# Two graph layers in float32: attention with the sources on the partitions, layer 0 as (attn @ h) @ W, one batch per group

## The chip, the cores and the metric

The kernel runs on one core of a Trainium2 chip. The time is that of the device, in microseconds, from launch to end. All data are float32. A core has TensorE (PE, matmuls; PEld is its weight load), VectorE (DVE), ScalarE (ACT), GpSimd (POOL) and SyncE (SP, here only the issue of DMAs). Each engine works through its own queue in order and waits at semaphores.

## The reference

x is 64 batches of 256 nodes with 512 features; adj (256 x 256) is shared by all batches. Both layers are pre-norm with a residual.

```python
# layer 0
h = relu(layernorm(x))
Wh = h @ W                                              # 512 x 512
logits = (Wh @ a_src)[:, :, None] + (Wh @ a_dst)[:, None, :]
logits = where(logits >= 0, logits, 0.2 * logits)
attn = softmax(where(adj == 0, -inf, logits))           # over the sources
x = x + attn @ Wh
# layer 1, 8 heads of 64
h = relu(layernorm(x))
q, k, v = h @ Wq.T + bq, h @ Wk.T + bk, h @ Wv.T + bv
attn = softmax(where(adj == 0, -inf, q @ k.T / 8))      # per head
x = x + (attn @ v) @ Wo.T + bo
```

## The kernel before

A group is two batches, i.e. four tiles of 128 tokens (`GB = 2`, L53). Everything stays on chip between load and store.

`norm_relu_T` (L121) takes mean and variance on VectorE, raises to the power -0.5 on GpSimd (L132), normalises on VectorE (xn, L137), transposes on TensorE (pt, L142) and applies relu on ScalarE (hT, L143). `project_rows` (L150) and `project_T` (L157) are the dense products: four accumulating matmuls, each with 512 moving columns.

`layer0` makes Wh (pw, copied to wh), its two row products with a_src and a_dst on VectorE (junk, L174), the logits with the targets on the partitions (z, L190 to L193), the row maximum, exp with the row sum (L200), transposes the probabilities (pp, L214) and multiplies them with wh (po, L223).

`layer1` makes qT and kT with the features on the partitions and v with the tokens on them. Then, for each tile of 128 targets and each four heads, `scores` multiplies qT by kT (psc, L281; a head has 64 features, so even and odd heads lie on the two halves of the rows), adds the mask and takes the row maximum on VectorE (s, L292), and takes exp with the row sum on ScalarE (pr, L308). `values` transposes the four probabilities (pp, L322), copies them back (pT, L327 and L329) and multiplies each with 64 columns of v (pav, L333). `finish` divides by the row sum (rc, L344; av, L346), transposes again (pa, L354, aT, L356), multiplies with Wo and stores.

Order: the generators of `layer1(g)` and `layer0(g + 1)` are interleaved step by step (L391 to L394), and a scheduler at build time orders the instructions of each engine, TensorE's too, by priority and its own estimate of when they are ready. SP issues first the load of x for group 0 and then those of the weights. PSUM's eight banks are split 2 (dense products), 3 (transposes) and 3 (scores).

Of the kernel before, what the change touches and what calls it, by code (L numbers as in the profile page):

```python
# [1 line left out]

# [13 lines left out]
P = 128  # L16
# [4 lines left out]
FLOOR = -1.0e30  # L21


@with_exitstack
def kernel(
# [17 lines left out]
    """Two pre-norm residual layers over batches of N nodes, kept on chip between them:  # L43
    graph attention with additive logits, then masked multi-head attention.

    A group is two batches, i.e. NT = 4 tiles of 128 tokens; its first layer is issued
    among the second layer of the group before it.
    """
# [4 lines left out]
    GB = 2  # L53
# [8 lines left out]
    big = ctx.enter_context(tc.tile_pool(name="big", bufs=2))  # L62
    work = ctx.enter_context(tc.tile_pool(name="work", bufs=3))
    small = ctx.enter_context(tc.tile_pool(name="small", bufs=4))
    ps_mm = ctx.enter_context(tc.tile_pool(name="ps_mm", bufs=2, space=PSUM))
    ps_tr = ctx.enter_context(tc.tile_pool(name="ps_tr", bufs=3, space=PSUM))
    ps_sc = ctx.enter_context(tc.tile_pool(name="ps_sc", bufs=3, space=PSUM))
# [3 lines left out]

    def load_group(g):
        xt = big.tile([P, NT, D], F32, tag="x", name=f"x_{g}", bufs=3)
        src = x_rows[g * TOK : (g + 1) * TOK, :].rearrange("(t p) d -> p t d", p=P)
        for t in range(0, NT, 2):
            nc.sync.dma_start(xt[:, t : t + 2, :], src[:, t : t + 2, :])
        return xt

    groups = {0: load_group(0)}
# [17 lines left out]
    make_identity(nc, ident)  # L97
    minus_half = const.tile([P, NT], F32, tag="minus_half", name="minus_half")
# [3 lines left out]
    a_src_b = load_row(a_src, "a_src_b")  # L102
    a_dst_b = load_row(a_dst, "a_dst_b")
# [8 lines left out]
    bv_b = load_row(bv, "bv_b")  # L112
    bo_b = load_row(bo, "bo_b")

    # 0 where there is an edge, MASKED where there is none
    mbias = const.tile([P, NC, N], F32, tag="mbias", name="mbias")
    nc.vector.tensor_scalar(mbias, adj_sb, 0.0, MASKED, op0=ALU.is_equal, op1=ALU.mult)
# [3 lines left out]
    def norm_relu_T(xt, g, layer):  # L121
        """relu(layernorm(x)) with the features on the partitions: [P, DC, TOK]."""
        nm = f"{layer}_{g}"
        mv = small.tile([P, NT, 2], F32, tag="mv", name=f"mv{nm}")
        for t in range(NT):
            st = small.tile([P, 6], F32, tag="st", name=f"st{nm}_{t}")
            nc.vector.bn_stats(st, xt[:, t, :])
            nc.vector.bn_aggr(mv[:, t, :], st)
        ve = small.tile([P, NT], F32, tag="ve", name=f"ve{nm}")
        nc.vector.tensor_scalar_add(ve, mv[:, :, 1], EPS)  # L130
        rstd = small.tile([P, NT], F32, tag="rstd", name=f"rstd{nm}")
        nc.gpsimd.tensor_tensor(rstd, ve, minus_half, op=ALU.pow)  # L132
        yield
        hT = big.tile([P, DC, TOK], F32, tag="hT", name=f"hT{nm}")
        for t in range(NT):
            xn = work.tile([P, D], F32, tag="xn", name=f"xn{nm}_{t}")
            nc.vector.tensor_scalar(  # L137
                xn, xt[:, t, :], mv[:, t, 0:1], rstd[:, t : t + 1], op0=ALU.subtract, op1=ALU.mult
            )
            pt = ps_tr.tile([P, DC, P], F32, tag="tr", name=f"pt{nm}_{t}")  # L140
            for c in range(DC):
                nc.tensor.transpose(pt[:, c, :], xn[:, c * P : (c + 1) * P], ident)  # L142
            nc.scalar.activation(hT[:, :, t * P : (t + 1) * P], pt, AF.Relu)  # L143
            yield
        return hT

    def project_rows(dst, hT, w_t, t):
        """dst[tokens of tile t, all columns] = h @ w_t"""
# [5 lines left out]
    def project_T(dst, hT, w_t, e):  # L154
        """dst[columns of chunk e, all tokens] = (h @ w_t).T"""
# [5 lines left out]
    def layer0(g):  # L161
        xt = groups[g]
        hT = yield from norm_relu_T(xt, g, 0)

        wh = big.tile([P, NT, D], F32, tag="wh", name=f"wh_{g}")
        es = small.tile([P, NT], F32, tag="es", name=f"es_{g}")
        ed = small.tile([P, NT], F32, tag="ed", name=f"ed_{g}")
        for t in range(NT):
            pw = ps_mm.tile([P, D], F32, tag="mm", name=f"pw_{g}_{t}")
            project_rows(pw, hT, w_sb, t)  # L170
            nc.scalar.copy(wh[:, t, :], pw)  # L171
            for dst, a in ((ed, a_dst_b), (es, a_src_b)):
                junk = work.tile([P, D], F32, tag="junk", name=f"junk_{g}_{t}", bufs=2)
                nc.vector.scalar_tensor_tensor(  # L174
                    junk, wh[:, t, :], 1.0, a, op0=ALU.mult, op1=ALU.mult, accum_out=dst[:, t : t + 1]
                )
            yield

        prob, rec = {}, {}
        for b in range(GB):  # L180
            per = ps_tr.tile([P, N], F32, tag="tr", name=f"per_{g}_{b}")
            for c in range(NC):
                t = b * NC + c
                nc.tensor.transpose(
                    per[:, c * P : (c + 1) * P], ed[:, t : t + 1].to_broadcast([P, P]), ident
                )
            z = work.tile([P, NC, N], F32, tag="z", name=f"z_{g}_{b}", bufs=2)
            for c in range(NC):
                t = b * NC + c
                nc.vector.scalar_tensor_tensor(  # L190
                    z[:, c, :], per, es[:, t : t + 1], mbias[:, c, :], op0=ALU.add, op1=ALU.add
                )
            nc.vector.scalar_tensor_tensor(z, z, NEG_SLOPE, z, op0=ALU.mult, op1=ALU.max)  # L193
            nmx = small.tile([P, NC], F32, tag="nmx0", name=f"nmx0_{g}_{b}")
            nc.vector.tensor_reduce(nmx, z, AX.X, ALU.max)
            nc.vector.tensor_scalar(nmx, nmx, FLOOR, -1.0, op0=ALU.max, op1=ALU.mult)
            pr = work.tile([P, NC, N], F32, tag="pr0", name=f"pr0_{g}_{b}", bufs=2)
            sm = small.tile([P, NC], F32, tag="sm0", name=f"sm0_{g}_{b}")
            for c in range(NC):
                nc.scalar.activation(  # L200
                    pr[:, c, :], z[:, c, :], AF.Exp, bias=nmx[:, c : c + 1], accum_out=sm[:, c : c + 1]
                )
            # a row without an edge gives 0
            nc.vector.tensor_scalar_max(sm, sm, 1e-30)
            rc = small.tile([P, NC], F32, tag="rc0", name=f"rc0_{g}_{b}")
            nc.vector.reciprocal(rc, sm)
            prob[b], rec[b] = pr, rc
            yield

        for b in range(GB):  # L210
            pp = ps_tr.tile([P, NC, N], F32, tag="tr", name=f"pp0_{g}_{b}")
            for mc in range(NC):
                for c in range(NC):
                    nc.tensor.transpose(  # L214
                        pp[:, mc, c * P : (c + 1) * P], prob[b][:, c, mc * P : (mc + 1) * P], ident
                    )
            pT = work.tile([P, NC, N], F32, tag="pT0", name=f"pT0_{g}_{b}", bufs=2)
            nc.vector.tensor_copy(pT, pp)
            for c in range(NC):
                t = b * NC + c  # L220
                po = ps_mm.tile([P, D], F32, tag="mm", name=f"po0_{g}_{t}")
                for mc in range(NC):
                    nc.tensor.matmul(  # L223
                        po,
                        pT[:, mc, c * P : (c + 1) * P],
                        wh[:, b * NC + mc, :],
                        start=(mc == 0),
                        stop=(mc == NC - 1),
                    )
                nc.vector.scalar_tensor_tensor(  # L230
                    xt[:, t, :], po, rec[b][:, c : c + 1], xt[:, t, :], op0=ALU.mult, op1=ALU.add
                )
            yield

    def layer1(g):
        xt = groups.pop(g)
        hT = yield from norm_relu_T(xt, g, 1)
        for t in range(NT):
            nc.gpsimd.tensor_tensor(xt[:, t, :], xt[:, t, :], bo_b, op=ALU.add)

        qT = big.tile([P, DC, TOK], F32, tag="qT", name=f"qT_{g}", bufs=1)
        kT = big.tile([P, DC, TOK], F32, tag="kT", name=f"kT_{g}", bufs=1)
        v = big.tile([P, NT, D], F32, tag="v", name=f"v_{g}")
        for e in range(DC):
            pq = ps_mm.tile([P, TOK], F32, tag="mm", name=f"pq_{g}_{e}")
            project_T(pq, hT, wq_sb, e)
            nc.scalar.activation(
                qT[:, e, :], pq, AF.Identity, bias=bqs_c[:, e : e + 1], scale=SCALE
            )
            pk = ps_mm.tile([P, TOK], F32, tag="mm", name=f"pk_{g}_{e}")  # L250
# [174 lines left out]
```

## Time and profile before

| | |
|---|---|
| median of 3 runs | 3981.32 us (3980.46 to 3982.46) |
| span of the profiled execution | 3978.6 us |
| TensorE busy | 3853.1 us, 97% |
| VectorE busy | 1732.9 us, 44% |
| ScalarE busy | 1109.1 us, 28% |
| GpSimd busy | 247.8 us, 6% |
| mean granted TensorE clock | 0.998 |
| HBM | 40.11 MB read, 33.55 MB written, 19 GB/s over the span |

The profile is of one execution; its span runs from the first to the last instruction and is 2.7 us shorter than the median. Matmuls are pipelined, so the duration of one (592 ns for 512 columns) is longer than the distance between the starts of two; a price is read from starts, not from durations. A float32 matmul leaves two records, a transpose one.

### The profile page before, as it was taken

How to read it: one execution, taken by the hardware profiler on the slowest of the kernel's cores; microseconds unless marked ns; L12 is line 12 of the kernel's file. 1: busy time of each engine (PE TensorE's matmuls, PEld its weight loads, DVE VectorE, ACT ScalarE, POOL GpSimd, SP SyncE). 2: the span in 40 equal slices, each digit the busy share in tenths (PEclk: the TensorE clock that was granted, in tenths of full speed). 3: DMA queues.
4: the chain of work that ended last, by engine and by line, in shares of the span. 5: the costliest groups of instructions: out<-in, count | busy, mean ns of one | idle time of the engine just before them, and what ended most of it. 6: DMA issues, size and time to landing. Idle time of an engine off the chain costs nothing.

```text
span 3978.6 us, 41676 instructions
## 1 busy us (share of the span) xinstructions
PE 3853.1 (97%) x15744; PEld 2182.8 (55%) x15744; DVE 1732.9 (44%) x5186; ACT 1109.1 (28%) x3201; POOL 247.8 (6%) x206
## 2 busy tenths in 40 slices
PE   7999999999999999999999999999999999999999
PEld 3555555555555555555555555555555555555555
DVE  3444344443345433454334543344443444433442
ACT  1322223222233222332223322233222232222332
POOL 1000000000000000000000000000000000000000
PEclk9999999999999999999999999999999999999999
DMA  2000000000000000000000000000000000000000
GB/s 98 22 9 16 19 22 22 9 16 19 22 22 14 13 17 22 22 22 6 19 19 22 22 6 19 19 22 22 9 16 19 22 22 9 16 19 22 11 11 11
DMA packets 39144, 76.33 MB, mean 19 GB/s; under 512 B 3297, under 2 KB 3297, under 8 KB 38945
## 3 DMA queue, kind: packets, MB, share of 16 engines
q1 hardware_dynamic: 38480, 72.36, 5.0%
q8 instruction: 124, 2.03, 0.2%
q0 software_dynamic: 464, 1.32, 0.1%
q14 instruction: 76, 0.61, 0.1%
HBM read 40.11 MB, written 33.55 MB: 19 GB/s over the span
## 4 chain that ended last, share of the span: by engine, by line
PE 87%; DVE 9%; ACT 3%; issue 1%; DMA 0%; POOL 0%; POOLq 0%; DVEq 0%; ACTq 0%
PE pav L333 12%; PE po L150 12%; PE pq L157 11%; PE pw L150 11%; PE pv L150 11%; PE pk L157 11%; PE psc L281 5%; PE pp L322 5%; PE po L223 4%; ACT hT L143 2%; PE pa L354 2%; DVE s L292 2%; PE pt L142 2%; DVE av L346 2%; DVE x L230 1%; DVE junk L174 1%
## 5 line engine op out<-in xcount | busy, mean ns | idle before, releaser
L333 PEld LDWEIGHTS pav<-v,pT 128*128 128x128 f32 x4096 | 498.8, 191 | 136.5 <-issue 45.9
L308 ACT ACTIVATE pr<-s,nmx 128x256 f32<-128x256 f32 x1024 | 507.0, 497 | 180.1 <-DVE nmx L304 157.9
L333 PE MATMUL pav<-v,pT 128*128 128x64 f32 x4096 | 525.0, 276 | 6.9 <-DVE pT L329 4.8
L150 PE MATMUL po<-wo_sb,aT 128*128 128x512 f32 x1024 | 474.2, 606 | 3.2 <-ACT aT L356 0.7
L157 PE MATMUL pq<-hT,wq_sb 128*128 128x512 f32 x1024 | 463.6, 595 | 7.9 <-ACT hT L143 7.9
L157 PE MATMUL pk<-hT,wk_sb 128*128 128x512 f32 x1024 | 460.3, 592 | 0.0
L150 PE MATMUL pw<-w_sb,hT 128*128 128x512 f32 x1024 | 460.1, 592 | 0.0
L150 PE MATMUL pv<-wv_sb,hT 128*128 128x512 f32 x1024 | 444.7, 592 | 0.0
L252 DVE TENSOR_SCALAR kT<-pk,bk_c 128x512 f32<-128x512 f32 x128 | 96.1, 751 | 776.0 <-PE pk L157 776.0
L281 PE MATMUL psc<-kT,qT 64*128 64x256 f32 x2048 | 399.0, 413 | 8.4 <-DVE mx L292 6.4
L292 DVE CUSTOM_DVE_ANT_0 s<-psc,mbias 128x256 f32<-128x256 f32 x1024 | 384.3, 417 | 11.1 <-PE psc L281 6.8
L171 ACT COPY wh<-pw 128x512 f32<-128x512 f32 x128 | 74.9, 585 | 1100.2 <-PE pw L150 1100.2
L157 PEld LDWEIGHTS pk<-hT,wk_sb 128*128 128x128 f32 x1024 | 194.6, 190 | 244.9 <-issue 244.9
L150 PEld LDWEIGHTS pv<-wv_sb,hT 128*128 128x128 f32 x1024 | 194.6, 190 | 244.9 <-issue 244.9
L150 PEld LDWEIGHTS pw<-w_sb,hT 128*128 128x128 f32 x1024 | 194.7, 190 | 244.5 <-issue 244.5
L157 PEld LDWEIGHTS pq<-hT,wq_sb 128*128 128x128 f32 x1024 | 191.9, 190 | 245.2 <-issue 229.6
L322 PE MATMUL pp<-ident,pr 128*128 128x128 f32 x2048 | 311.6, 277 | 5.0
L327 ACT COPY pT<-pp 128x512 f32<-128x512 f32 x256 | 149.1, 582 | 581.1 <-PE pp L322 578.2
L150 PEld LDWEIGHTS po<-wo_sb,aT 128*128 128x128 f32 x1024 | 184.4, 190 | 217.3 <-issue 184.1
L322 PEld LDWEIGHTS pp<-ident,pr 128*128 128x128 f32 x2048 | 234.3, 145 | 83.6 <-issue 44.1
L281 PEld LDWEIGHTS psc<-kT,qT 64*128 64x128 f32 x2048 | 220.9, 185 | 100.1 <-issue 56.8
L174 DVE SCALAR_TENSOR_TENSOR junk<-wh,a_dst_b 128x512 f32<-128x512 f32 x128 | 88.5, 691 | 421.4 <-ACT wh L171 421.4
(57 smaller groups left out, 3103.3 us busy)
## 6 DMA issues: line engine op xcount, KB each, us to landing
x<-in_x_dram SPq DMA_DIRECT2D x64, 512.0 KB, 4.4
out_dram<-x SPq DMA_DIRECT2D x128, 256.0 KB, 2.0
w_sb<-in_L_gnn_W_dram SPq DMA_DIRECT2D x1, 1024.0 KB, 13.3
wq_sb<-in_L_gnn_Wq_dram SPq DMA_DIRECT2D x1, 1024.0 KB, 15.9
wk_sb<-in_L_gnn_Wk_dram SPq DMA_DIRECT2D x1, 1024.0 KB, 18.1
wv_sb<-in_L_gnn_Wv_dram SPq DMA_DIRECT2D x1, 1024.0 KB, 20.1
wo_sb<-in_L_gnn_Wo_dram SPq DMA_DIRECT2D x1, 1024.0 KB, 16.1
a_src_b<-in_L_gnn_a_src_dram POOLq DMA_DIRECT2D x1, 256.0 KB, 6.8
```

The costliest lines, as they stand in the source:

```text
L142: nc.tensor.transpose(pt[:, c, :], xn[:, c * P : (c + 1) * P], ident)
L150: nc.tensor.matmul(dst, hT[:, c, t * P : (t + 1) * P], w_t[:, c, :], start=(c == 0), stop=(c == DC - 1))
L157: nc.tensor.matmul(dst, w_t[:, c, e * P : (e + 1) * P], hT[:, c, :], start=(c == 0), stop=(c == DC - 1))
L174: nc.vector.scalar_tensor_tensor(junk, wh[:, t, :], 1.0, a, op0=ALU.mult, op1=ALU.mult, accum_out=dst[:, t : t + 1])
L223: nc.tensor.matmul(po, pT[:, mc, c * P : (c + 1) * P], wh[:, b * NC + mc, :], start=(mc == 0), stop=(mc == NC - 1),)
L252: nc.vector.tensor_scalar_add(kT[:, e, :], pk, bk_c[:, e : e + 1])
L281: nc.tensor.matmul(psc[r][:, i, :], qT[rows, e, t * P : (t + 1) * P], kT[rows, e, b * N : (b + 1) * N], start=True, stop=True,)
L292: nc.vector.tensor_tensor_reduce(out=s[:, j, :], in0=psc[r][:, i, :], in1=mbias[:, c, :], scale=1.0, scalar=FLOOR, op0=ALU.add, op1=ALU.ma ...
L308: nc.scalar.activation(pr[:, j, :], s[:, j, :], AF.Exp, bias=nmx[:, j : j + 1], accum_out=sm[:, h : h + 1])
L322: nc.tensor.transpose(pp[:, r, kc, :], pr[:, 2 * i + r, kc * P : (kc + 1) * P], ident)
L327: nc.scalar.copy(pT, pp)
L333: nc.tensor.matmul(pav[:, h * DH : (h + 1) * DH], pT[:, r, kc, :], v[:, b * NC + kc, h * DH : (h + 1) * DH], start=(kc == 0), stop=(kc == ...
```

## The change

- A group is one batch (`GB = 1`, 64 groups); the dense products with features on the partitions have 256 moving columns, those with tokens on them 512 as before.
- Layer 0: h keeps its tokens on the partitions. Its row products are taken with W @ a_src and W @ a_dst, which are made once. exp(leaky_relu(s + d)) is the larger of exp(s)exp(d) and exp(0.2 s)exp(0.2 d), so only vectors go through exp (xs, xd) and VectorE builds the matrix (e1, eb), sources on the partitions. GpSimd multiplies by the transposed mask (em) and adds the two halves (esum); a product with ones sums over the sources. uT = (attn @ h) transposed is the product of h and em, scaled by the reciprocal of the sums, and W comes last.
- Layer 1: scores are made with the sources on the partitions. No maximum is subtracted: exp on ScalarE straight from PSUM, times the mask on VectorE (pm), the two halves added on GpSimd (sm). `values` has v as the stationary operand and pm as the moving one, 256 columns; even heads go to rows 0 to 63 of the output and odd heads to 64 to 127, and the sums over the sources come from a product with ones into the same rows of another bank (psm). VectorE takes the reciprocal of 512 sums and multiplies. The result is already transposed for Wo. The bias bv is folded into bo once.
- A bound is computed from the weights (`constants`): powers of the heads' Gram matrices of Wq and Wk, the sizes of biases and of W @ a. It gives a flag, which goes through DRAM into a register; where it says that the bound doesn't hold, `general` computes everything again with row maxima, batch by batch.
- TensorE's instructions keep the order in which the program writes them (`manual_schedule`); the other engines are still ordered by the scheduler. The order is that of a planner over three generators: at each step it takes the stage with the smallest key, group + done/cost + offset. A yield carries the cost of its TensorE work.
- x of group 0 is loaded after the weights in SP's order. PSUM: four banks for dense products and transposes, two for scores, one each for pav and psm.

The core of the diff; new functions that the prediction doesn't need in full are cut.

```diff
+GB = 1
...
-    GB = 2
...
+        ps_mm = ctx_b.enter_context(tc.tile_pool(name="ps_mm", bufs=4, space=PSUM))
+        ps_sc = ctx_b.enter_context(tc.tile_pool(name="ps_sc", bufs=2, space=PSUM))
+        ps_av = ctx_b.enter_context(tc.tile_pool(name="ps_av", bufs=1, space=PSUM))
...
+        def layer0(g):
...
+            pe = bank([P, TOK], f"pe_{g}")
+            for t in range(NT):
...
+                    pe[:, t * P : (t + 1) * P], es[:, t : t + 1].to_broadcast([P, P]), ident
+                )
+            xs = work.tile([P, 2, TOK], F32, tag="xs", name=f"xs_{g}")
+            xd = small.tile([P, 2, NT], F32, tag="xd", name=f"xd_{g}")
+            for j, slope in enumerate((1.0, NEG_SLOPE)):
+                nc.scalar.activation(xd[:, j, :], ed, AF.Exp, scale=slope)
+                nc.scalar.activation(xs[:, j, :], pe, AF.Exp, scale=slope)
+            yield 0.25
...
+                    nc.vector.tensor_scalar_mul(e1, xs[:, 0, cols], xd[:, 0, t : t + 1])
+                    nc.vector.scalar_tensor_tensor(
+                        eb[:, m, :], xs[:, 1, cols], xd[:, 1, t : t + 1], e1, op0=ALU.mult, op1=ALU.max
+                    )
+                em[b] = work.tile([P, NC, N], F32, tag="em", name=f"em_{g}_{b}")
+                nc.gpsimd.tensor_tensor(em[b], eb, maskT, op=ALU.mult)
+                esum[b] = work.tile([P, N], F32, tag="esum", name=f"esum_{g}_{b}")
+                nc.gpsimd.tensor_tensor(esum[b], em[b][:, 0, :], em[b][:, 1, :], op=ALU.add)
+                yield 0.0
...
+            ps = bank([P, TOK], f"ps_{g}")
+            for b in range(GB):
+                nc.tensor.matmul(
+                    ps[:, b * N : (b + 1) * N], ones, esum[b], start=True, stop=True
+                )
+            nc.vector.tensor_scalar_max(rs, ps, 1e-38)
+            nc.vector.reciprocal(rs, rs)
+            yield 0.45
...
+                    yield 1.7
+            for t in range(NT):
+                po = bank([P, D], f"po0_{g}_{t}")
+                project_rows(po, uT, w_sb, t)
+                nc.vector.tensor_add(xt[:, t, :], po, xt[:, t, :])
+                yield 3.43
...
+        def attention(g):
...
+            def scores(b, e):
...
+                for m in range(NC):
+                    for r in range(2):
+                        rows = slice(r * DH, (r + 1) * DH)
+                        nc.tensor.matmul(
+                            psc[r][:, m, :],
+                            kT[rows, e, b * N + m * P : b * N + (m + 1) * P],
+                            qT[rows, e, b * N : (b + 1) * N],
...
+                for r in range(2):
+                    nc.scalar.activation(ex[:, r, :, :], psc[r], AF.Exp)
+                pm = work.tile([P, 2, NC, N], F32, tag="pm", name=f"pm_{g}_{b}_{e}")
+                for r in range(2):
+                    nc.vector.tensor_mul(pm[:, r, :, :], ex[:, r, :, :], maskT)
+                sm = work.tile([P, 2, N], F32, tag="sm", name=f"sm_{g}_{b}_{e}")
+                nc.gpsimd.tensor_tensor(sm, pm[:, :, 0, :], pm[:, :, 1, :], op=ALU.add)
...
+            def values(b, e):
+                pm, sm = probs.pop((b, e))
+                i = e % 2
...
+                for m in range(NC):
+                    for r in range(2):
+                        h = 2 * e + r
+                        nc.tensor.matmul(
+                            pav[r * DH : (r + 1) * DH, i, :],
+                            v[:, b * NC + m, h * DH : (h + 1) * DH],
+                            pm[:, r, m, :],
...
+                for r in range(2):
+                    nc.tensor.matmul(
+                        psm[r * DH : (r + 1) * DH, i, :],
+                        ones[:, 0:DH],
+                        sm[:, r, :],
...
+                if i == 0:
+                    return
...
+                rc = work.tile([P, 2, N], F32, tag="rc", name=f"rc_{g}_{b}_{e}")
+                nc.vector.reciprocal(rc, psm)
+                nc.vector.tensor_mul(aTs[b][:, e - 1 : e + 1, :], pav, rc)
...
+            for n, unit in enumerate(units):
+                scores(*unit)
+                yield 0.9
+                if late:
+                    late.pop(0)()
+                    yield 1.3 if n == 0 else 3.43
+                if n:
+                    values(*units[n - 1])
+                    yield 1.3
+            late.append(partial(values, *units[-1]))
+            late.extend(partial(finish, t) for t in range(NT))
...
+        stages = [
+            [layer0, 11.5, 0.0],
+            [projections, 21.5, 1.1],
+            [attention, 15.7, 2.2],
+        ]
+        state = [dict(g=0, gen=None, done=0.0) for _ in stages]
+        side = constants()
+        while any(s["g"] < G for s in state):
+            keys = []
+            for k, s in enumerate(state):
+                if s["g"] < G and (k == 0 or state[k - 1]["g"] > s["g"]):
+                    keys.append((s["g"] + s["done"] / stages[k][1] + stages[k][2], k))
+            _, k = min(keys)
+            s = state[k]
+            if s["gen"] is None:
+                s["gen"], s["done"] = stages[k][0](s["g"]), 0.0
+            cost = next(s["gen"], None)
+            if cost is None:
+                s["g"], s["gen"], s["done"] = s["g"] + 1, None, 0.0
+            else:
+                s["done"] += cost
...
+    with ExitStack() as ctx_b:
+        with tc.manual_schedule(engines={mybir.EngineType.PE}):
+            bounded()
+    flag_dram = dram.tile([1, 1], I32, tag="flag_dram", name="flag_dram")
+    nc.sync.dma_start(flag_dram, flag)
+    unproven = nc.values_load(flag_dram[0:1, 0:1], min_val=0, max_val=1)
+    with tc.If(unproven > 0):
+        with ExitStack() as ctx_g:
+            general()
```

`projections` runs the norm, the transposes pt, then q and k by turns in steps of 1.72 and v in steps of 3.43; its last pt and its first q follow one another.

## The prediction

> **What bounds the kernel now.** I read the page's busy line and chain first, then TensorE's timeline in one steady group, then single tiles.
>
> ```profile
> PE 3853.1 (97%) x15744; PEld 2182.8 (55%) x15744; DVE 1732.9 (44%) x5186; ACT 1109.1 (28%) x3201; POOL 247.8 (6%) x206
> PE 87%; DVE 9%; ACT 3%; issue 1%; DMA 0%; POOL 0%; POOLq 0%; DVEq 0%; ACTq 0%
> ```
>
> TensorE is busy 97% of 3978.6 us and is 87% of the chain. VectorE at 44% is far from being a bound, so the price list of TensorE counts. Its timeline (start, us, operation, count; two records per float32 matmul, one per transpose):
>
> ```profile
> 2006.99 1.09 PE L322 MATMUL pp<-ident,pr 128*128 128x128 f32 x8
> 2008.02 0.70 PE L281 MATMUL psc<-kT,qT 64*128 64x256 f32 x4
> 2008.65 2.00 PE L333 MATMUL pav<-v,pT 128*128 128x64 f32 x16
> 2010.58 0.70 PE L281 MATMUL psc<-kT,qT 64*128 64x256 f32 x4
> ...
> 2035.24 3.60 PE L157 MATMUL pk<-hT,wk_sb 128*128 128x512 f32 x8
> 2038.67 3.60 PE L157 MATMUL pq<-hT,wq_sb 128*128 128x512 f32 x8
> ```
> ```profile
> 59.97 3.70 PE L157 MATMUL pq<-hT,wq_sb 128*128 128x512 f32 x8 [0.23 <-ACT hT L143]
> ...
> 115.10 1.13 PE L281 MATMUL psc<-kT,qT 64*128 64x256 f32 x8
> 116.16 0.43 PE L184 MATMUL per<-ident,ed 128*128 128x128 f32 x2
> ```
> ```profile
> 3878.51 3.70 PE L157 MATMUL pq<-hT,wq_sb 128*128 128x512 f32 x8 [0.79 <-ACT hT L143]
> ```
>
> From start to start: 8 records of 512 columns take 3.43 us, **0.429 us** a record; so a 256-column record is 0.215 (half, an estimate). Transposes cost 1.03/8 = 0.13, elsewhere 0.11. A 64-column record costs 1.93/16 = **0.12**, not 0.054: moving only 64 columns wastes half. Scores on half the rows: four matmuls (8 records) take 116.16 - 115.10 = **1.06 us**, five units of 0.213 where one after another would be eight; two halves run beside each other, except that the first and the last record stand alone. The group period is (3878.51 - 59.97)/31 = 123.2 us, **61.6 us per batch**.
>
> **What the skill says.** "VectorE: DVE Perf Modes", First, the fixed hardware budget: reciprocal is an iterative divide with a repeat count of 8. The trace agrees: two elements take 156 ns and eight 202, so (202 - 156)/6 = 7.7 ns each, where other operations of 2 or 4 elements (L196, L304) differ by under 10.
>
> ```profile
> L344 DVE RECIPROCAL rc<-sm x128: 189/202/204, 128.7 to 3963.1; 128x8 f32<-128x8 f32 x128
> L206 DVE RECIPROCAL rc<-sm x64: 152/156/166, 36.8 to 3827.0; 128x2 f32<-128x2 f32 x64
> ```
>
> "TensorE: Matmul & The Clock Gate", What's actually happening: an idle window of about 3.4 us halves TensorE's clock, and a busy one restores it. The trace agrees (columns: window, length, TensorE busy, granted clock, DMA): idle from 32.1 to 36.12 but for one short transpose before, the clock falls at 33.9 and is back only at 40.7, 4.5 us after work resumed.
>
> ```profile
> 33.00:34.00 1.00, 0.00 (x0) 0.92 0.00 0
> ...
> 36.00:37.00 1.00, 0.86 (x3) 0.50 0.03 8
> ...
> 39.00:40.00 1.00, 1.00 (x2) 0.50 0.00 0
> 40.00:41.00 1.00, 1.00 (x3) 0.67 0.00 0
> ```
>
> The same page, Part 3, says that matmuls on separate column groups also run concurrently. No column group occurs in this trace; rows agree.
>
> **The change on TensorE, per batch.** Removed: the transposes of the probabilities (pp, pp0) and of av (pa), and 64-column matmuls.
> - Layer 0: 2 transposes 0.25; row sums 0.43; attn@h, 8 matmuls of 256 columns, 16 x 0.215 = 3.44; times W, 16 x 0.429 = 6.86. Sum 11.0.
> - Projections: 8 transposes 1.0; q and k, 64 records x 0.215 = 13.8; v 6.86. Sum 21.7.
> - Attention, four units. Scores: the shape measured above, 1.06. Values: six matmuls alternating between two column halves. Not shown before: if they pair as the row halves do, seven units of 0.213 = 1.49; perfect pairing gives 1.28, none 2.56. I take 1.49. Output 6.86. Sum 4 x 2.55 + 6.86 = 17.1.
> - Switching between shapes: entering a dense stream costs about 0.1 (2031.70 to 2035.24 is 3.54 for the first block, 3.43 for the next). Some ten entries: 1.0 (0 to 2).
>
> Together **50.8 us** against 61.6. If TensorE never waited, 64 batches would take 64 x 50.8 = 3251.
>
> **The waits it adds.** TensorE's order is now written by the planner, and TensorE is served in order. I followed its rule (smallest progress key) by hand through a period. It repeats: values of unit 1 (VA1), then at once the two transposes `pe` of a later batch, at once the row sum `ps`, then scores of unit 3, pu, pt, values of unit 2, pt, q. The zero-cost yields change no key, so nothing goes between `pe` and `ps`. But `ps` needs pe -> exp (ScalarE) -> e1, eb (VectorE) -> em, esum (GpSimd). Behind it are queued all matmuls of other stages, ready as they are.
>
> And VA1 ends with a reciprocal of 512 elements, which is written earlier and ready earlier than e1, so it stands first in VectorE's queue: 0.16 + 510 x 7.7 ns = 4.1 us. From VA1's end: pipeline and semaphore 0.25; reciprocal to 4.35; product with pav, 0.65 (row of av, L346, less its overlap with the next), to 5.0; two e1 and two eb of 256 elements, 1.5 together (between half of xn, L137, 0.54, and z, L190, 0.476), to 6.5; em on GpSimd at the row of L239, 1.39, to 7.95; esum, half as large, 0.75, to 8.7. Less `pe`'s own 0.25, TensorE idles **8.4 us** (7.7 if e1 goes before the product). ScalarE's exps, some 1.0 us, lie under the reciprocal. Without the reciprocal in front it is 0.25 + 1.3 + 1.2 (last eb after the last exp) + 2.2 = 4.9.
>
> An idle of 8.4 contains a whole window, so the clock halves. Work restarts at half speed for about 4.5 us (measured above): it loses **2.2**.
>
> Then q waits for relu after pt: `pq` waits 0.23 to 0.79 for hT now, once per two batches; pt and q are now adjacent in every batch: 0.85 (pipeline 0.25 and relu 0.6, L143).
>
> What I cost at nothing: unit 3's and 0's evacuations and masks; each has 6 to 19 us of TensorE work before its reader. VA3's reciprocal is hidden by 8 us (q, scores, po0, k) before `fin0`. The single pav and psm banks are free before VA2 because the gap itself covers them; without the gap this wait, some 1 us, appears. VectorE's sum rises to some 32 us per batch: masks 8 x 0.65 = 5.2, reciprocals 2 x 4.1 + 2.1 = 10.3, products 2.9, junk and statistics about 6, evacuations and the rest 8. That is half of 61, no bound, and GpSimd's 12 us neither (seven operations of 1.39, a half one, two pow of 1.0).
>
> **Ends.** x of batch 0 is now issued on SP behind five weights of 1 MB; at some 400 GB/s (windows from 15 to 25 us) it lands near 19 us instead of 4.6. Then statistics and pow 3, h and junk 3, the pe-ps chain 5, rs 3, pu's products 1.5, po0 7: layer 0 of batch 0 ends near 43. Constants: 3.4 (bias) + about 12 (Gram products) + 8 of small dependent waits = 23, once. Last attention alone, bound by exp, mask and reciprocals, loses some 13 us; flag to DRAM, its load and the branch some 8 (4 to 15, nothing shown): 21. With the reference's weights the tested sums are 0.31 against 0.66, 0.95 against 1.95 and 0.36 against 1, so the general path isn't taken.
>
> **The sum.** 43 + (64 x 50.8 - 11 = 3240, layer 0 of batch 0 being in the 43) + 23 + 21 + 63 x 0.85 = 3381; each us of gap in a batch adds 63. Gap 8.4 and clock 2.2: 63 x 10.6 = 668, **4049** of span. The span before, 3978.6, stands 2.7 below the median 3981.3; adding it, **4052**. Per batch: 62.3 against 61.6, what the matmuls gain is spent on waiting. This case's own range is 3930 to 4160 (gap 7 to 9.5, switching 0 to 2, values 1.28 to 1.7). It turns faster below gap plus clock = (3978.6 - 3381)/63 = 9.5 us.
>
> **Rivals.**
> 1. *Shorter gap, faster.* One mechanism: e1 and eb don't stand behind a slow reciprocal, because 512 elements stream faster than eight suggest, or VectorE's queue has them in front. Gap 4.9, clock lost in some of the batches, 1.0: 3381 + 63 x 5.9 = 3753, with 2.7 3756. It decides from a reciprocal below about 3.1 us. For it: only 2 and 8 elements were seen. Against: the slope agrees with the page.
> 2. *No gap.* TensorE's order isn't as I read it, and other stages fill the wait: 3381 + 3, about 3384. Against: TensorE's order is set by hand, and the rule leaves no room.
> 3. *Column halves don't overlap.* 256 units x 1.07 = 274 more: 4326. For it: no column group shown; against: row halves overlap.
> 4. *General path taken*: several times longer; the sums above exclude it.
>
> **Chances.** Forecast 0.58, rival 1 0.20, rival 2 0.10, rival 3 0.12. Measurement can tell about 0.2% (3973 to 3989) from no change. Of the forecast's 0.58, its range lies 0.39 above, 0.04 within, 0.15 below. Slower 0.39 + 0.12 = 0.51, same 0.04, faster 0.15 + 0.20 + 0.10 = 0.45. The range 3670 to 4290 leaves out rival 2, half of rival 3 and small tails, 0.2.
>
> **What would show it.** `ps` waiting 8 us for esum in each batch, and the clock at 0.5 behind it; RECIPROCAL of 512 elements near 4.1 us; six records of `values` starting in pairs, 1.5 us per unit; `pq` waiting about 0.85 for hT. I am wrong if TensorE is busy over 95%, if the reciprocal takes under 3 us, or if values take 2.5.

## The result

The changed kernel takes 4003.45 us (median of 4 runs, 3999.38 to 4005.06) against 3980.89 us. The ratio is 1.0051, with a 95% interval of 1.0036 to 1.0065: slower by half a per cent, 22.6 us. The forecast was 4052 us, with a range of 3930 to 4160. The mechanism was right, and the size of the change was not: the forecast rise of 71 us is three times the measured one. The side came out right too, but partly by luck, because two errors opposed each other (see below).

### The profile page after: what moved, and what is told of

Read it like the earlier page. It is cut to its first block, busy times and chain, and to the rows that moved or that the text cites. A ratio compares the mean times of both kernels' runs of the same rounds, so it can differ in the third digit from the quotient of the medians.

```text
span 3997.5 us, 35588 instructions
## 1 busy us (share of the span) xinstructions
PE 3462.0 (87%) x14222; PEld 2086.4 (52%) x14222; DVE 1981.7 (50%) x3186; ACT 707.4 (18%) x1428; POOL 723.8 (18%) x657
## 4 chain that ended last, share of the span: by engine, by line
PE 85%; DVE 8%; POOL 3%; issue 1%; ACT 1%; DMA 0%; SPq 0%; POOLq 0%; DVEq 0%
PE po L125 22%; PE pq L132 12%; PE pk L132 11%; PE pv L125 11%; PE psc L420 8%; PE pu L344 7%; PE pav L448 7%; DVE rc L468 5%; PE psm L456 3%; POOL em L324 2%; PE ps L333 2%; PE pt L379 2%; DVE eb L320 2%; POOL esum L326 1%; ACT hT L380 1%
## 5 line engine op out<-in xcount | busy, mean ns | idle before, releaser
L433 POOL TENSOR_TENSOR sm<-pm 128x512 f32<-128x512 f32 x256 | 324.9, 1269 | 2430.2 <-DVE pm L431 1320.5
L468 DVE RECIPROCAL rc<-psm 128x512 f32<-128x512 f32 x128 | 429.8, 3358 | 255.2 <-PE psm L456 255.2
L431 DVE TENSOR_TENSOR pm<-ex,maskT 128x512 f32<-128x512 f32 x512 | 331.6, 689 | 432.2 <-ACT ex L428 432.2
L132 PE MATMUL pq<-hT,wq_sb 128*128 128x256 f32 x2048 | 503.7, 389 | 44.1 <-ACT hT L380 44.1
L132 PE MATMUL pk<-hT,wk_sb 128*128 128x256 f32 x2048 | 490.6, 382 | 0.0
L125 PE MATMUL po<-w_sb,uT 128*128 128x512 f32 x1024 | 466.6, 598 | 0.0
L333 PE MATMUL ps<-esum,ones 128*128 128x256 f32 x128 | 77.6, 709 | 447.7 <-POOL esum L326 444.0
L428 ACT ACTIVATE ex<-psc 128x512 f32<-128x512 f32 x512 | 278.0, 594 | 941.7 <-PE psc L420 941.7
L420 PE MATMUL psc<-qT,kT 64*128 64x256 f32 x2048 | 347.3, 465 | 0.0
L344 PE MATMUL pu<-em,h 128*128 128x256 f32 x1024 | 299.7, 442 | 0.0
L448 PE MATMUL pav<-pm,v 128*64 128x256 f32 x2048 | 280.5, 395 | 10.3 <-DVE aT L469 10.3
```

What stands on the lines that cost most here:

```text
L125: nc.tensor.matmul(dst, hT[:, c, t * P : (t + 1) * P], w_t[:, c, :], start=(c == 0), stop=(c == DC - 1))
L132: nc.tensor.matmul(dst, w_t[:, c, e * P : (e + 1) * P], hT[:, c, :], start=(c == 0), stop=(c == DC - 1))
L333: nc.tensor.matmul(ps[:, b * N : (b + 1) * N], ones, esum[b], start=True, stop=True)
L344: nc.tensor.matmul(pu[:, d, :], h[:, b * NC + m, (dp + d) * P : (dp + d + 1) * P], em[b][:, m, :], start=(m == 0), stop=(m == NC - 1),)
L420: nc.tensor.matmul(psc[r][:, m, :], kT[rows, e, b * N + m * P : b * N + (m + 1) * P], qT[rows, e, b * N : (b + 1) * N], start=True, stop=True,
L428: nc.scalar.activation(ex[:, r, :, :], psc[r], AF.Exp)
```

## The profile after

Busy time of the engines and the chain that ended last:

```profile
PE 3462.0 (87%) x14222; PEld 2086.4 (52%) x14222; DVE 1981.7 (50%) x3186; ACT 707.4 (18%) x1428; POOL 723.8 (18%) x657
PE 85%; DVE 8%; POOL 3%; issue 1%; ACT 1%; DMA 0%; SPq 0%; POOLq 0%; DVEq 0%
```

TensorE is busy 391 us less than before, and yet the span is 19 us longer (3997.5 against 3978.6). So the work did shrink, and TensorE stands idle for what was saved. What it waited for, in total, times and longest:

```profile
PE ps L333 <- POOL esum L326: 444.0, 63, 7.2
PE pq L132 <- ACT hT L380: 44.1, 64, 0.7
PE pav L448 <- DVE aT L469: 10.3, 3, 3.6
```

Two waits matter, each once per batch; every other one is 10.3 us or less in all. The timeline of one period of TensorE shows the place, as the planner's rule had given it: VA1, `pe`, wait, `ps`, scores, pu, pt, VA2, pt, wait, q.

```profile
2006.48 1.22 PE L333 MATMUL ps<-esum,ones 128*128 128x256 f32 x2 [7.18 <-POOL esum L326]
...
2058.86 1.08 PE L448 MATMUL pav<-pm,v 128*64 128x256 f32 x8
2059.78 0.60 PE L456 MATMUL psm<-sm,ones 128*64 128x256 f32 x4
2060.31 0.43 PE L303 MATMUL pe<-ident,es 128*128 128x128 f32 x2
2067.93 1.22 PE L333 MATMUL ps<-esum,ones 128*128 128x256 f32 x2 [7.19 <-POOL esum L326]
2069.08 2.08 PE L420 MATMUL psc<-qT,kT 64*128 64x256 f32 x8
2071.09 2.65 PE L344 MATMUL pu<-em,h 128*128 128x256 f32 x8
...
2076.89 1.99 PE L132 MATMUL pq<-hT,wq_sb 128*128 128x256 f32 x8 [0.69 <-ACT hT L380]
2078.82 1.13 PE L420 MATMUL psc<-qT,kT 64*128 64x256 f32 x8
```

The period is 67.93 - 6.48 = 61.45 us per batch, where the kernel before has 61.6. By starts, TensorE idles from 2060.57 (2060.31 and two transposes of 0.13) to 2067.93: **7.36 us**. The scores behind it take 2.01 us from start to start and those at 2078.82 1.06, which is the half clock. And this is what the other engines do meanwhile:

```profile
2060.42 3.36 DVE L468 RECIPROCAL rc<-psm 128x512 f32<-128x512 f32 x1 [2.85 <-PE psm L456]
2060.78 0.66 ACT L310 ACTIVATE xs<-pe 128x256 f32<-128x256 f32 x2 [1.22 <-PE pe L303]
2063.70 0.25 DVE L319 TENSOR_SCALAR e<-xs,xd 128x256 f32<-128x256 f32 x1
2063.87 0.68 DVE L469 TENSOR_TENSOR aT<-pav,rc 128x512 f32<-128x512 f32 x1
2064.47 0.48 DVE L320 SCALAR_TENSOR_TENSOR eb<-xs,xd,e 128x256 f32<-128x256 f32 x1
2064.86 0.35 DVE L319 TENSOR_SCALAR e<-xs,xd 128x256 f32<-128x256 f32 x1
2065.24 0.48 DVE L320 SCALAR_TENSOR_TENSOR eb<-xs,xd,e 128x256 f32<-128x256 f32 x1
2065.81 1.26 POOL L324 TENSOR_TENSOR em<-eb,maskT 128x512 f32<-128x512 f32 x1 [11.23 <-DVE eb L320]
2067.15 0.72 POOL L326 TENSOR_TENSOR esum<-em 128x256 f32<-128x256 f32 x1
```

The exps xs end at 2061.44 and would be ready for VectorE; VectorE is inside the reciprocal until 2063.78. The wait's name in the list, esum, is only the last link. The granted clock of TensorE in the same places (window, length, busy, clock):

```profile
2053.00:2060.50 7.50, 7.50 (x28) 1.00 0.30 76
2060.50:2067.90 7.40, 0.24 (x2) 0.85 0.07 29
2067.90:2072.50 4.60, 4.57 (x14) 0.51 0.02 4
2072.50:2076.00 3.50, 3.50 (x26) 1.00 0.00 0
```

## Experiments

The theory is that of the forecast: TensorE serves its queue in the written order, `ps` waits there for a chain that begins behind a long reciprocal, and the clock behind the wait is half. The rivals: TensorE's work is the bound after all; VectorE's sum of work is; the wait comes from the exps and GpSimd whatever the reciprocal does. Gains and losses per batch are differences to the changed kernel's 4003.45 us, divided by 63. Ratios are to the kernel before, with 95% intervals.

### The order alone

Two kernels change nothing but the planner's numbers. No instruction is added or removed. The first:

```diff
                 nc.gpsimd.tensor_tensor(esum[b], em[b][:, 0, :], em[b][:, 1, :], op=ALU.add)
-                yield 0.0
+                yield 3.0
...
-            [layer0, 11.5, 0.0],
+            [layer0, 14.5, 0.0],
```

> Only the planner's cost numbers change: the step between em and ps counts 3.0 instead of 0, layer 0 in all 14.5 instead of 11.5, so that scores of unit 3, pt, values of unit 2, pt, q and scores of unit 0 stand between pe and ps. No instruction is added or taken away. Theory (the order of TensorE alone makes the wait and the half clock): the 7.4 and 2.2 us go, but values of unit 2 now come about 1.8 us behind values of unit 1 and wait some 2.4 us for their banks: 61.4 - 9.6 + 2.4 = 54.2 us per batch, about 3550 us. Rival (the time is in the work and the wait would only move to another place): above 3900 us.

Measured: 3576.7 us, ratio 0.898 (0.8965 to 0.8995), 27 us from the expected value and 427 us faster than the changed kernel. The new wait, too, is the one that was expected, 2.4 us in each batch, for the single banks of pav and psm:

```profile
PE pav L448 <- DVE aT L469: 148.8, 63, 3.6
```

The second kernel spaces this apart as well:

```diff
-                yield 0.0
+                yield 2.5
...
-                yield 0.44
+                yield 0.44 if t < NT - 1 else 2.0
...
-            [layer0, 11.5, 0.0],
-            [projections, 21.5, 1.1],
-            [attention, 15.7, 2.2],
+            [layer0, 14.0, 0.0],
+            [projections, 23.06, 1.3],
+            [attention, 15.7, 2.6],
```

> Again only the planner's numbers: ps counts 2.5 behind em, the last pt 2.0 behind its relu, the stages' sums follow, and the offsets are 1.3 and 2.6 instead of 1.1 and 2.2. By the rule, followed by hand, pe and ps then stand over 9 us apart, units 1 and 2 8 us, the last pt and the first q 3 us. Theory: all steady waits go, 61.44 - 7.4 - 2.2 - 0.7 = 51.1 us per batch, 63 x 10.3 = 649 us less: about 3355 us, faster than both kernels. Rival (waiting moves to VectorE's queue): above 3600 us.

Measured: **3366.1 us, ratio 0.8451 (0.8437 to 0.8465)**, faster than both kernels. Its busy line, and VA1 to `ps` in a period:

```profile
PE 3308.9 (98%) x14222; PEld 2011.2 (60%) x14222; DVE 1984.2 (59%) x3186; ACT 687.3 (20%) x1428; POOL 725.3 (22%) x657
```
```profile
2033.91 0.38 PE L303 MATMUL pe<-ident,es 128*128 128x128 f32 x2
2034.39 3.70 PE L125 MATMUL pv<-wv_sb,hT 128*128 128x512 f32 x8
2038.02 1.08 PE L448 MATMUL pav<-pm,v 128*64 128x256 f32 x8
2038.93 0.60 PE L456 MATMUL psm<-sm,ones 128*64 128x256 f32 x4
...
2047.50 0.59 PE L333 MATMUL ps<-esum,ones 128*128 128x256 f32 x2
```

`ps` now starts 13.6 us behind `pe` and waits for nothing here; the period, from one `ps` (2047.50) to the next (2098.64), is 51.14 us, where 51.1 was expected. VectorE works as long as in the changed kernel (1984 against 1982 us), so its sum did not bound the changed kernel. TensorE's work did not either, for it is the same work. This settles the main question: the order cost (4003.45 - 3366.11)/63 = 10.1 us per batch.

### The reciprocal, by its place

Computed twice, with `if e == 1:` (the end of unit 1) in one kernel and `if e == 3:` in the other:

```diff
                 nc.vector.reciprocal(rc, psm)
+                if e == 1:
+                    nc.vector.reciprocal(rc, psm)
```

> The reciprocal of the 512 sums is computed twice where unit 1 ends, just ahead of pe: 3.36 us more on VectorE per batch. Theory (this reciprocal stands in front of e1 and eb, on the path to ps): ps starts 3.36 us later in every batch, 64 x 3.36 = 215 us more, about 4215 us. Rival (the wait is set by the exps and by GpSimd, not by the reciprocal): under 20 us more.

> The same reciprocal is computed twice where unit 3 ends, 8.2 us of TensorE work ahead of its reader fin0. Theory (a reciprocal costs by its place, not by its length): two of 3.36 us and the product, 7.6 us with the start, still fit into 8.2; within 10 us of the changed kernel's 4003 us. Rival (VectorE's sum, half the span, sets the pace): about 215 us more, as with unit 1.

Measured: 4223.84 us (1.0608, 1.059 to 1.0626), i.e. 220 us more than the changed kernel, and 4016.5 us (1.0083, 1.0066 to 1.01), 13 us more. In front of e1 the second reciprocal costs 3.5 us a batch. Behind unit 3, where 8.2 us of matmuls stand before its reader, it costs nothing in the steady batches: the first and the last `ps` start at 33.3 and 3851.0 us, in the changed kernel at 33.9 and 3850.3. What is added lies behind the last `ps`, where fewer matmuls are left to hide it; `po` waits for it three times:

```profile
PE po L125 <- DVE aT L471: 12.6, 3, 5.9
```

The 13 us are 3 beyond the margin I had given, but a fifteenth of the rival's 215.

And left out at unit 1:

```diff
+                if e == 1:
+                    nc.vector.tensor_copy(rc, psm)
+                else:
+                    nc.vector.reciprocal(rc, psm)
-                nc.vector.reciprocal(rc, psm)
```

> Leaves out the reciprocal where unit 1 ends: a copy of the sums takes its place, so heads 0 to 3 are multiplied by their sums and not divided by them. A copy takes 0.69 us where the reciprocal takes 3.36. Theory: ps waits for the exps instead, 4.9 us in place of 7.4; 2.5 us less per batch, and part of the half clock: between 63 x 2.5 = 158 us less (3845 us) and 63 x 4.7 = 300 us less (3705 us). If the clock's recovery falls on its windows of 3.41 us, the period goes from 18 windows, 61.44 us, to 17, 58.0: 3788 us. Rival (GpSimd and the exps set the wait): 4003 us.

Measured: 3852.48 us (0.9675, 0.9659 to 0.9691), 151 us less, just short of the 158 to 300 expected; the 3788 us of the variant with 17 windows fell. The wait of `ps`:

```profile
PE ps L333 <- POOL esum L326: 299.3, 63, 5.1
```

It is (444.0 - 299.3)/63 = 2.3 us shorter, so the reciprocal was in the chain, and what stays, 4.95 us by starts, is the chain of exps, products and GpSimd. The forecast had put it at 4.9, though without the product with pav, which here stands in the chain. But the gain per batch, 151/63 = 2.4 us, is only the wait; the clock loss did not shrink with it, against the forecast for this case (1.0 instead of 2.2).

### The clock behind the wait

Matmuls that nobody reads fill the wait:

```diff
                 nc.scalar.activation(xs[:, j, :], pe, AF.Exp, scale=slope)
+            dummy = bank([P, D], f"dummy_{g}")
+            for c in range(2 * DC):
+                nc.tensor.matmul(dummy, ones, w_sb[:, c % DC, :], start=True, stop=True)
             yield 0.25
```

> Eight matmuls of 512 columns whose result nobody reads are added between pe and ps in every batch: about 6.9 us of extra TensorE work, inside the wait of 7.4 us. Theory (the wait holds TensorE's queue, and the half clock behind it costs 2.2 us a batch on top): the clock stays at 1.0, ps starts no later, and the kernel gets faster by 63 x 2.2 = 140 us, to about 3860 us, with 440 us more of matmuls in it. Rival (the clock behind the wait is hidden by other waits): 4000 us, as the changed kernel. Rival (TensorE's work is the bound): 4003 + 440 = 4440 us.

Measured: 3877.02 us (0.9736, 0.9719 to 0.9752), faster than the changed kernel by 126 us and than the kernel before, with an estimated 440 us more of matmuls in it (64 batches of 16 records of 0.429).

```profile
2060.92 0.43 PE L303 MATMUL pe<-ident,es 128*128 128x128 f32 x2
2061.18 7.03 PE L313 MATMUL dummy<-w_sb,ones 128*128 128x512 f32 x16
2068.54 0.70 PE L336 MATMUL ps<-esum,ones 128*128 128x256 f32 x2 [0.32 <-POOL esum L329]
```

The distance from `pe` to `ps` is unchanged (7.62 us), only the clock is kept: 126.4/63 = **2.0 us** per batch is the price of the half clock, where 2.2 was expected. The mean clock is 0.995 against 0.942. The changed kernel's own clock lines agree: 4.6 us at 0.51 behind the wait lose 4.6 x 0.49 = 2.25 us.

### Wait and clock loss do not add up

The 61.45 us were suspicious. "TensorE: Matmul & The Clock Gate", What's actually happening, in the Trainium skill gives the clock's window as 3413 ns and says that it runs freely; 61.44 is 18 of these. The traces agree: in the steady batches every stretch at half clock lasts a whole number of windows, 6.83 us in the changed kernel (two) and 10.24 with the shorter wait below (three), and begins within the wait. If every batch has one half-clock stretch that ends on this raster, the distance between two such ends can only be a whole number of windows, and a somewhat shorter or longer wait changes the length of the stretch instead of the period. Two kernels shift the wait a little:

```diff
-                nc.vector.reciprocal(rc, psm)
+                if e == 1:
+                    nc.vector.reciprocal(rc[:, 0, :], psm[:, 0, :])
+                    nc.vector.reciprocal(rc[:, 1, 0:64], psm[:, 1, 0:64])
+                    nc.vector.tensor_copy(rc[:, 1, 64:N], psm[:, 1, 64:N])
+                else:
+                    nc.vector.reciprocal(rc, psm)
```
```diff
+                if e == 1:
+                    nc.vector.reciprocal(rc[:, 0, 0:48], psm[:, 0, 0:48])
                 nc.vector.reciprocal(rc, psm)
```

> Leaves out a part of the division where unit 1 ends: 192 of its 512 sums are copied and not inverted, so some heads 2 and 3 are multiplied by their sums. VectorE needs some 0.8 us less ahead of e1. Theory (the clock comes back only on a raster of 3.41 us, and the period locks to 18 of them, 61.44 us, as long as the work without any half clock and the wait together, 59.2 us, leave between 1.7 and 3.4 us for the loss): the wait shrinks by 0.8 us and the half clock lasts 1.6 us longer; the time stays within 10 us of the changed kernel's 4003 us. Rival (wait and clock loss add up): 63 x 0.8 = 50 us less, 3953 us.

> 48 sums are inverted once more where unit 1 ends, ahead of the whole reciprocal: some 0.42 us more in front of e1. Theory of the raster: the half clock gets 0.8 us shorter, the period stays at 61.44 us; within 10 us of 4003 us. Rival (wait and clock loss add up): 63 x 0.42 = 26 us more, 4030 us.

Measured: 3993.09 us (1.0026, 1.0016 to 1.0036) and 4007.85 us (1.0063, 1.0049 to 1.0076). With the shorter wait (0.9 us: 7.36 to 6.46 by starts) the kernel gains 10 us and not 54; with the longer one (0.46 us: 473.2 against 444.0 in all) it loses 4 and not 29. The shorter wait, by timeline and by clock:

```profile
2004.37 1.22 PE L333 MATMUL ps<-esum,ones 128*128 128x256 f32 x2 [6.29 <-POOL esum L326]
2059.09 0.43 PE L303 MATMUL pe<-ident,es 128*128 128x128 f32 x2
2065.81 1.22 PE L333 MATMUL ps<-esum,ones 128*128 128x256 f32 x2 [6.29 <-POOL esum L326]
```
```profile
2065.80:2072.50 6.70, 6.69 (x20) 0.53 0.02 4
```

The period is 61.44 as before, and the half clock behind the wait lasts some 6.3 us (0.53 over 6.7) where it lasted 4.5 (0.51 over 4.6); 1.6 longer was expected, 1.8 came. The mean clock fell from 0.942 to 0.918 as the wait got shorter. So the 10 and the 4 us are not in the steady period. The raster also fits the two coarser edits: (4223.84 - 4003.45)/63 = 3.5 us is about one window more, and without the reciprocal the ends of the half clock lie 17, 17 and 18 windows apart in turn, 59.2 us on average, where (4003.45 - 3852.48)/63 = 2.4 gives 59.0. That the clock changes only on this raster is read from the traces; that one number of windows holds over a range of waits is argued from it, and only these waits were tried.

The clock also says why the shorter wait brought no shorter loss. In the changed kernel (first two lines) it falls after some 5 us of idle, with the shorter wait (last two) after 2.6, one window earlier:

```profile
2060.60:2065.60 5.00, 0.14 (x2) 1.00 0.09 34
2065.60:2067.90 2.30, 0.00 (x0) 0.50 0.00 0
...
2059.30:2061.90 2.60, 0.22 (x2) 1.00 0.23 89
2061.90:2065.80 3.90, 0.00 (x0) 0.50 0.00 0
```

So the fall needs no idle window of 3.4 us, as the prediction had it; here the measurement decides. In the first kernel of "The order alone" the clock falls even in waits of 2.3 us, in every third or fourth batch. At 2066.10 TensorE has waited from 2063.91 on:

```profile
2066.10:2069.40 3.30, 3.18 (x14) 0.50 0.00 0
```

In the changed kernel and its nine variants the clock fell at the end of windows in which the profile has TensorE busy for up to 45%, and stayed after windows with 48% or more (an estimate, since the ends of matmuls are modelled). In the two kernels with the old order it also fell after some windows of 74 to 77%; what counts there stays open.

### The column halves

> The kernel with the spaced order (3366 us), but values finishes one column half before it begins the other: the same matmuls, two neighbours of the same half behind one another. Theory (column halves run beside each other only where they alternate): the eight records of pav take seven units of 0.213 instead of five, psm is unchanged; 256 x 0.43 = 109 us more, 3475 us. Rival (halves do not overlap in float32, and the short times have another reason): 3366 us.

The edit, on the kernel with the spaced order:

```diff
-                for m in range(NC):
-                    for r in range(2):
+                for r in range(2):
+                    for m in range(NC):
                         h = 2 * e + r
```

Measured: 3369.92 us (0.8462, 0.8449 to 0.8475), 4 us more. My expectation fell. A unit of values in this kernel:

```profile
2013.53 1.09 PE L448 MATMUL pav<-pm,v 128*64 128x256 f32 x8
2014.44 0.61 PE L456 MATMUL psm<-sm,ones 128*64 128x256 f32 x4
2014.98 1.99 PE L132 MATMUL pq<-hT,wq_sb 128*128 128x256 f32 x8
```

Twelve records take 1.45 us whether the halves alternate or not. Single starts in the trace show why the sum came out: in both kernels records start in pairs, some 6 and 13 ns apart, a pair every 0.216 us; the first pair takes some 0.05 more. That is six units and the entry, not seven units. The scores likewise start in pairs 6 ns apart; the first pair takes 0.31, so the prediction's reading of their 1.06 us (first and last record alone) had the right length and the wrong parts. Whether a pair of `values` is one record of each half, or the two records of one matmul, the trace does not name, and no run separates the two; the first was forecast and is not shown. The scores, on row halves, are settled by the lone ones in the next section.

### One batch per group by itself

`GB = 1` in the kernel before, nothing else.

> The kernel before with one batch per group, nothing else of the change. Theory (the column count of the dense products is free as long as it is 256 or more): the same TensorE work, and the wait of the first q for relu, 0.2 to 0.8 us, comes 64 times instead of 32: 10 to 60 us more than 3981. Rival (256 columns pay more per record, and one batch offers too little work to fill in between): over 150 us more.

Measured: 4188.5 us (1.0517, 1.05 to 1.0535), 208 us more; my theory fell. The columns are not the reason: eight records of 256 columns take 1.73 us in its timeline, half of 3.43.

```profile
PE pa L354 <- DVE av L346: 111.2, 128, 1.1
PE pq L157 <- ACT hT L143: 19.4, 63, 0.7
```

The waits sum to 197 us against 109 before, and the mean clock of 0.987 against 0.998 is 0.011 x 4186 = 46 us of full speed. The two together are at most 88 + 46 = 134 of 208. Most of the rest is in the scores, by their place. A score of one head alone:

```profile
2027.12 0.70 PE L281 MATMUL psc<-kT,qT 64*128 64x256 f32 x2
2027.74 0.44 PE L322 MATMUL pp<-ident,pr 128*128 128x128 f32 x2
```

It takes 0.62 us to the next start, its two records 0.32 apart, and two heads next to each other take 0.63 together (2008.02 to 2008.65 in the kernel before). The scheduler leaves 255 scores alone with one batch per group and 67 before; from start to start, without the waits, all scores take 447 us against 382, 65 us more. So two row halves run beside each other only where their matmuls are neighbours in the order. In the changed kernel this loss doesn't show: its eight records of scores always stand together.

## Why the forecast was right in kind and wrong in size

Per batch, with what was measured in place of each step:

| step | forecast | measured |
|---|---|---|
| TensorE's work with switching | 50.8 | 51.4 (61.44 less idle, half clock of 2.0 and q); 51.1 in the spaced kernel |
| idle before `ps` | 8.4 | 7.36 |
| of it the reciprocal of 512 | 4.1 | 3.36 |
| half clock behind it | 2.2 | 2.0 (2.25 by the clock lines) |
| q waits for relu | 0.85 | 0.69 |
| period | 62.3 | 61.44 |

The difference of 0.8 us, 63 times, is the 51.5 us between the forecast span of 4049 and 3997.5.

**The step that failed** is "0.16 + 510 x 7.7 ns = 4.1 us". The price per element came from the rows of 2 and 8 elements. The changed kernel has two longer rows:

```profile
L337 DVE RECIPROCAL rs<-rs x64: 1742/1753/1754, 36.1 to 3851.4; 128x256 f32<-128x256 f32 x64
L468 DVE RECIPROCAL rc<-psm x128: 3351/3358/3359, 138.7 to 3983.6; 128x512 f32<-128x512 f32 x128
```

3.36 us for 512 and 1.75 for 256: (3358 - 1753)/256 = 6.3 ns each. (Read from PSUM, as rc is, 256 take 1.76 in the kernel with the shorter wait, so the source is not the reason.) The prediction took its 7.7 as agreeing with the page's repeat count of 8; at these lengths the measurement decides. The 0.74 us too many are most of the 1.04 by which the idle was too long, and 47 of the 51.5 us by the forecast's own sum. The sum was a difference of two nearly equal numbers, 62.3 and 61.6, so 1.3% of the time became a factor of three in the change. That one term nearly closes the account is partly chance, because the others cancel: the rest of the idle, the clock and q were 0.3, up to 0.2 and 0.16 us too high and TensorE's work 0.3 to 0.6 too low.

The side was partly luck for the same reason. With the measured idle, q and half clock (2.0 to 2.25) the forecast's sum, 3381 - 63 x 0.16 + 63 x (7.36 + 2.0 or 2.25), gives 3961 to 3976 us of span, a little less than the 3978.6 before; only the work that it had too low brings the changed kernel back above it.

**A second step failed**, the rule that each us of gap adds 63: 0.9 us less brought 10 us instead of 54, and 0.46 us more cost 4 instead of 29. So the 47 us are the forecast's arithmetic. What a reciprocal of 4.1 us would have cost in this kernel was not run; it lies between 0.46 us more, where the period stays, and 3.36 more, where it grows by one window.

**Right** were: the order of TensorE, stage by stage; the reciprocal in front of e1; the half clock; the pq wait; the shapes' prices; that VectorE and GpSimd are no bound in sum; that a bank wait of VA2 appears once the gap is gone, though it is 2.4 us and not some 1. The first e went ahead of the product (2063.70 before 2063.87), but eb only behind it, so the product's 0.6 us stayed in the chain. At the ends, layer 0 of batch 0 was done at 46.8 instead of 43, and 3.6 us lie behind the last addition where I had put 8 for the flag; these cancel. Rival 1's shorter gap was seen in the kernel without the reciprocal: its wait of 4.9 came out, by another sum, and its clock loss of 1.0 did not. Rival 2 (no gap) describes the kernel with the spaced order, 3366 against its 3384. Rival 3 (no overlap in `values`) fell: a unit takes 1.45 us and not 2.56, whichever records pair. Rival 4 fell as well: the general path would have taken several times as long.

What the change brings on TensorE is therefore real, some 10.2 us per batch (61.6 to 51.4), and it went into one wait and the clock behind it. Where the planner counts TensorE's costs alone, it cannot see the latency of a chain through three other engines.

## What to carry to other kernels

When an engine's order is written by hand, go through one steady period and ask for every pair of neighbours how long the chain between them takes through the other engines, with the longest instruction that may stand ahead of it in each queue; a planner's zero-cost step is a wait. Price such an instruction from rows near its own size. And look at the clock in every wait of TensorE: here it fell in each steady wait of 4.95 us and more, and in some of 2.3. Fill such a wait or remove it altogether: shortening it a little may gain nothing.

## What the runs showed of the hardware that I had not expected

- A period with one half-clock stretch locks to a whole number of 3.41 us: 18 of them in four kernels whose waits range from 6.46 to 7.8 us, 19 with the doubled reciprocal, 17, 17, 18 in turn without it. A shorter wait can lower the mean clock (0.942 to 0.918).
- The clock falls without a whole idle window: after 2.2 us of idle in waits of 2.3, and with the changed kernel's order after windows busy for 45% or less.
- Matmuls of 64 columns on two halves of TensorE's columns need not alternate in the program: twelve records with 256 moving columns take 1.45 us in both orders, and they start in pairs.
- Two matmuls on the two row halves take 0.63 us together when they are neighbours, and one alone takes 0.62.
- The reciprocal costs 6.3 ns per element from 256 to 512 elements, less than the 7.7 between 2 and 8.
